# The softplus of a scan step as one ScalarE function on VectorE's copies, in a two-layer state-space and attention block

## The chip, the cores and the metric

The kernel runs on one core of a Trainium2 chip. The metric is the device time of one execution in microseconds (us), the median of several runs. The engines are TensorE (PE in the profile, PEld for its weight loads), VectorE (DVE), ScalarE (ACT), GpSimd (POOL) and SyncE (SP), which only issues DMAs. Each engine works through its own list of instructions in order and waits at an instruction until what it needs is done.

## The reference, cut to what matters

Eight images of 64x64 positions and 96 channels go through two layers. The first is a two-dimensional state-space scan, the second attention without softmax and a feed-forward layer in an emulated 8-bit format. The change lies in the first, in the step sizes of the scan:

```python
xz = x @ in_proj_w.T                               # 192 channels for the scan, 192 for the gate
xc = silu(depthwise 3x3 convolution of the first half)
xs = the image along diagonals and antidiagonals, each also backwards    # 4 directions
dts, Bs, Cs = split(einsum("bkdl,kcd->bkcl", xs, x_proj_weight), [6, 22])
delta = softplus(einsum("bkrl,kdr->bkdl", dts, dt_projs_weight) + dt_projs_bias)
A = -exp(A_logs)                                   # 4 directions x 192 channels x 16 states
def step(h, (u, d, B, C)):
    h = h * exp(d * A) + (d * u) * B               # for each of 16 states
    return h, sum over the states of h * C
y = scans of the four directions, put back into place and added
out = (layernorm(y) * silu(z)) @ out_proj_w.T
```

`delta` is `d`, and `delta * u` is the product that the kernel calls `du`. Softplus is ln(1 + exp(v)). The attention, the feed-forward layer and the norms are computed too, and are not touched.

## The kernel before, in words

**The steps.** A step is one image, one sense (`q`, forwards or backwards) and 512 positions of the scan; both directions of that sense share the 128 partitions, 64 channels each, and three groups (`G = 3`) cover the 192 channels. There are 8 images x 2 senses x 8 chunks = 128 steps. In a step the 16 states are 16 iterations, so the main loop has 2048 iterations; iteration `i` is state `n = i mod 16` of step `m`.

**An iteration.** `decay` makes exp(delta * A) on ScalarE, three activations (L1003), two iterations ahead, into three buffers. The input of the recurrence comes in one of two ways, by the string `FEED = "DADADADADADAAAAA"`. In a D iteration (n = 0, 2, 4, 6, 8, 10) TensorE spreads the row B over the partitions (L1027) and VectorE multiplies it by `du` (three products, L1042). In an A iteration (the other ten) ScalarE multiplies the transposed `du`, called `duT`, by B (eight activations, L1017), and TensorE turns the result (L1025). Both land in the three PSUM banks `feed`. VectorE then runs the recurrence, three scans of 512 positions (L1038). POOL keeps the last column (L1054) and multiplies by C (L1059), and TensorE transposes that product into a PSUM sum (L1073), four iterations after the scan. The `feed` banks are single: a bank is filled for the next iteration after its scan has read it.

**The prologue.** What a step needs beforehand is written by `prologue(m)`: the projections `rows` and `x` (L915 to L928), `delta`, `du` (L966) and `duT` (L971 to L973). It is started at iteration 13 of step m - 2 and runs, spread over the iterations of step m - 1, while that step is scanned. The softplus in it is ln(1 + exp(-|v|)) + max(v, 0): TensorE computes v (L938), ScalarE makes |v|, exp and ln (L940, L942, L945), POOL works out what the sum 1 + e lost by rounding and adds it to the logarithm (four passes, L949, L950, L952, L954), TensorE computes v a second time (L957), and VectorE adds max(v, 0) (L959). `du` has one buffer, so the product waits until iteration 10 of the step before has used its own for the last time.

**The other work.** Beside the scans run, as streams, `front` of the next image (norm, convolution, gate, walk along the diagonals) and `tail` of the last one (join, layer norm, attention, feed-forward). Prologues and streams are Python generators. Before each of their pieces they say which engine it is for and its price in us: `yield act(0.6)`, `dve`, `gp` for POOL, `pe`, and `bank` for TensorE with one of two PSUM banks. The planner `Work` grants each engine a credit an iteration (`PLACES`: ScalarE 2.0, VectorE 1.5, POOL 3.5, TensorE 0.85 three times) and lets a piece in while the credit lasts. A prologue is urgent: it goes in at once and may drive the credit below zero, and the streams then wait. A bank is kept from the streams while a prologue is waiting for one. `LAGS` says how many iterations later a piece may follow one on another engine. All of this is fixed when the program is built; on the chip the order of every engine is a fixed list.

**Tables.** ScalarE has exp and ln in one loaded set of tables. `silu` of the front belongs to another set, so each of its blocks is enclosed by two loads (L566 and, by `k.tables()`, L63).

Of the kernel before, what the change touches and what calls it, by code (L numbers as in the profile page):

```python
# [12 lines left out]
AF = mybir.ActivationFunctionType  # L13
ALU = mybir.AluOpType
# [3 lines left out]
P = 128  # L18
# [6 lines left out]
NR = 6  # L25
# [6 lines left out]
T = 512  # L32
NST = L // T
NSTEP = 2 * NST
TB = T // P
G = 3
# [11 lines left out]
FEED = "DADADADADADAAAAA"  # L48
# [196 lines left out]
def act(us, lag=None):  # L245
    return "A", us, lag, False


def dve(us, lag=None):
    return "V", us, lag, False  # L250


def gp(us, lag=None):
    return "G", us, lag, False


def pe(us, lag=None):
    return "P", us, lag, False


def bank(us, lag=None, long=False):

    return "P", us, lag, "long" if long else "short"
# [130 lines left out]
def view(b, p, *dims):  # L394

    n = int(np.prod(dims))
    v = b[0:p, 0:n]
    if len(dims) == 1:
        return v
    names = "abc"[: len(dims)]  # L400
    return v.rearrange(f"p ({' '.join(names)}) -> p {' '.join(names)}", **dict(zip(names, dims)))
# [458 lines left out]
def run(tc, psum, dram, x, out, w, NB):  # L860
# [9 lines left out]
    nc = tc.nc  # L870
# [24 lines left out]
    made, decays, feeds, hs, carry, sums, other = {}, {}, {}, {}, {}, {}, {}  # L895
    feed = [psum.tile([P, T], F32, tag=f"feed{g}", name=f"feed{g}") for g in range(G)]
    banks = [psum.tile([P, T], F32, tag=f"bank{i}", name=f"bank{i}") for i in range(2)]
    work = Work(banks + feed)

    def prologue(m):  # L900

        b, q, c = steps[m]
        o, u = made[m], made[m].u

        def tile(name, shape, bufs=2):
            return pool.tile(shape, F32, tag=name, name=f"{name}_{m}", bufs=bufs)


        ps = yield bank(1.0, 0)
        v = view(ps, P, TB, NX)  # L910
        for j in range(TB):
            if j == 2:
                yield pe(0.8)
            for g in range(G):
                nc.tensor.matmul(  # L915
                    v[:, j, :], u[:, g, j * P : (j + 1) * P], w.wx[:, q, g, :], start=(g == 0), stop=(g == G - 1)
                )
        yield act(0.45)
        rows = o.rows = tile("rows", [P, TB, NX])
        nc.scalar.copy(rows, v)  # L920
        work.release(ps)
        ps = yield bank(0.45)
        v = view(ps, NX, T)
        for j in range(TB):
            nc.tensor.transpose(v[:, j * P : (j + 1) * P], rows[:, j, :], w.ident)
        yield act(0.6)
        x = o.x = tile("x", [NX, T])
        nc.scalar.activation(x, v, AF.Identity, bias=w.xb)  # L928
        work.release(ps)
        o.crow = dram.tile([2 * NS, T], F32, tag="crow", name=f"crow_{m}", bufs=3)  # L930
        nc.sync.dma_start(out=o.crow, in_=x[XC:NX, :])

        e = tile("e", [P, G, T], 1)
        for g in range(G):
            ps = yield bank(0.85)
            nc.tensor.matmul(ps, w.ws[:, q, g, :], x[0 : 2 * NR + 1, :], start=True, stop=True)  # L938
            yield act(0.6)
            nc.scalar.activation(e[:, g, :], ps, AF.Abs)  # L940
            work.release(ps)
        nc.scalar.activation(e, e, AF.Exp, scale=-1.0)  # L942
        yield act(1.5, 1)
        delta = tile("delta", [P, G, T])
        nc.scalar.activation(delta, e, AF.Ln, bias=w.one)  # L945
        duT = tile("duT", [P, TB * G, P])
        f = duT.rearrange("p (g k) t -> p g (k t)", g=G)
        yield gp(3.0)
        nc.gpsimd.tensor_scalar(f, e, 1.0, 1.0, ALU.mult, ALU.add)  # L949
        nc.gpsimd.tensor_scalar(f, f, -1.0, 1.0, ALU.add, ALU.mult)  # L950
        yield gp(3.4, 1)
        nc.gpsimd.tensor_tensor(e, e, f, ALU.subtract)  # L952
        yield gp(3.4, 1)
        nc.gpsimd.tensor_tensor(delta, delta, e, ALU.add)  # L954
        for g in range(G):
            ps = yield bank(0.85)
            nc.tensor.matmul(ps, w.ws[:, q, g, :], x[0 : 2 * NR + 1, :], start=True, stop=True)  # L957
            yield dve(0.7)
            nc.vector.scalar_tensor_tensor(delta[:, g, :], ps, 0.0, delta[:, g, :], ALU.max, ALU.add)  # L959
            work.release(ps)  # L960
        o.delta = delta
        yield gp(3.4)
        while m and not made[m - 1].multiplied:
            yield "G", 0.0, -1, False
        du = o.du = tile("du", [P, G, T], 1)
        nc.gpsimd.tensor_tensor(du, delta, u, ALU.mult)  # L966
        for j in range(G):
            ps = yield bank(0.45)
            for i in range(4):
                r, g = divmod(4 * j + i, G)  # L970
                nc.tensor.transpose(ps[:, i * P : (i + 1) * P], du[:, g, r * P : (r + 1) * P], w.ident)  # L971
            yield act(0.6)
            nc.scalar.copy(duT[:, 4 * j : 4 * j + 4, :], view(ps, P, 4, P))  # L973
            work.release(ps)
        o.duT = duT

    def bring(m):

        b, q, c = steps[m]
        work.finish(lambda: c in image(b).walked)  # L980
        u = pool.tile([P, G, T], F32, tag="u", name=f"u_{m}", bufs=2)
        made[m] = SimpleNamespace(u=u, c={}, multiplied=False)
        for d in range(2):
            nc.sync.dma_start(
                out=u[d * GC : (d + 1) * GC],
                in_=image(b).seq[d][:, c * T : (c + 1) * T].rearrange("(g i) t -> i g t", i=GC),
            )
# [41 lines left out]
    def recur(i):  # L1029
        m, n = divmod(i, NS)  # L1030
        _, q, _ = steps[m]
        h = hs[i] = pool.tile([P, G, T], F32, tag="h", name=f"h_{i}", bufs=6)
        a = decays.pop(i)
        back = slice(None, None, -1) if q else slice(None)

        def scan(g):
            init = carry[m - 1][:, n, g : g + 1] if m % NST else 0.0
            nc.vector.tensor_tensor_scan(h[:, g, back], a[:, g, back], feed[g][:, back], init, ALU.mult, ALU.add)  # L1038

        if FEED[n] == "D":  # L1040
            for g in (1, 2, 0):
                nc.vector.tensor_tensor(feed[g], feed[0], made[m].du[:, g, :], ALU.mult)  # L1042
        if n == FEED.rindex("D"):
            made[m].multiplied = True
        scan(0)
        scan(1)
        work.at("V")
        scan(2)
# [108 lines left out]
    for m in range(2):  # L1157
        bring(m)
    work.start(prologue(0), urgent=True)
    work.hurry(lambda: not work.urgent)  # L1160

    work.kept = feed
    work.finish(lambda: all(any(f is x for x, _ in work.free) for f in feed))
    work.free = [f for f in work.free if any(f[0] is b for b in banks)]

    work.start(prologue(1), urgent=True)
    for tag, at in (("P", 2), ("A", 0), ("P", 2)):
        work.now += tag == "A"
# [12 lines left out]
    for i in range(total + LAG + 1):  # L1181
        m, n = divmod(i, NS)
# [17 lines left out]
        if i < total:  # L1200
            recur(i)
        else:
            work.at("V")
# [100 lines left out]
```

## Time and profile before

| what | value |
|---|---|
| median of 3 runs | 11828.1 us (11826.46 to 11834.27) |
| profiled execution, its own time | 11827.4 us |
| its span in the trace | 11825.6 us |
| mean granted clock of TensorE | 0.915 |
| first scan starts, last scan ends | 255.5 us, 11567.6 us |
| busy, share of the span: PE, DVE, ACT, POOL | 84%, 82%, 80%, 82% |
| four rounding passes on POOL (L949, L950, L952, L954), busy | 194.0 + 188.8 + 442.0 + 441.1 us |
| VectorE's part of the softplus (L959), busy and idle before it | 259.8 and 257.6 us |
| ScalarE's part (L940, L942, L945), busy | 224.0 + 190.2 + 200.0 us |
| second computation of v (L957), TensorE busy | 440.9 us |

Busy times of an engine are unions, so instructions that overlap count once. The idle time in front of an instruction is put down to what released it. A busy TensorE is not TensorE at its peak, since its matmuls overlap and their ends are modelled.

### The profile page before, as it was taken

The page shows a single profiled execution, that of the slowest core. Times are in us where ns is not written, and L with a number is a line of the kernel's source. Part 1 is how long each engine was busy: PE and PEld are TensorE (multiplying, and loading weights), DVE is VectorE, ACT ScalarE, POOL GpSimd, SP SyncE. Part 2 cuts the span into 40 slices and gives each one's busy share as a digit, 9 for nine tenths or more (in the row PEclk, how much of TensorE's full clock was granted, in tenths as well). Part 3 has the DMA queues.
Part 4 walks back from the last instruction along what each step waited for, and adds up shares of the span by engine and source line. Part 5 has one row for each costly group of instructions (what it writes and reads, how often), then busy time and mean ns, then how long its engine had stood idle before and what let it go on. Part 6 is the DMA issues. An engine that isn't in the chain of part 4 may idle for free.

```text
span 11825.6 us, 186556 instructions
## 1 busy us (share of the span) xinstructions
PE 9882.5 (84%) x62677; PEld 7958.3 (67%) x62677; DVE 9688.2 (82%) x11100; ACT 9489.7 (80%) x19827; POOL 9737.8 (82%) x6927
## 2 busy tenths in 40 slices
PE   6898889888898888888888888988889888888885
PEld 5677677666776667776677666766667666666664
DVE  2988988888888888888888888888888878878993
ACT  3888888878887788887888878887788878878883
POOL 1987988888978898888987889888898878979993
PEclk8999999998998989999898999999999999988996
DMA  3335332533335333353333433344333533332332
GB/s 88 101 93 137 99 93 89 138 107 99 91 93 142 104 95 92 100 136 100 92 96 105 126 101 98 92 118 120 98 92 91 136 104 93 101 92 82 95 96 58
DMA packets 1122756, 1207.21 MB, mean 102 GB/s; under 512 B 452789, under 2 KB 730006, under 8 KB 1121798
## 3 DMA queue, kind: packets, MB, share of 16 engines
q1 hardware_dynamic: 1121798, 1195.28, 36.8%
q8 instruction: 498, 8.16, 0.3%
q14 instruction: 460, 3.77, 0.1%
HBM read 874.83 MB, written 319.98 MB: 101 GB/s over the span
## 4 chain that ended last, share of the span: by engine, by line
PE 33%; DVE 21%; ACT 20%; POOL 11%; issue 8%; DMA 4%; SPq 3%; DVEq 0%; POOLq 0%; ACTq 0%
DVE h L1038 13%; PE y L1073 8%; PE feed L1025 8%; ACT feedT L1017 7%; POOL h L1059 6%; ACT decay L1003 5%; DVE feed L1042 5%; PE bank L550 4%; DMA cc<-crow 2%; PE bank L915 2%; PE bank L957 2%; SPq L595 2%; PE feed L1027 1%; POOL delta L954 1%; PE bank L938 1%
## 5 line engine op out<-in xcount | busy, mean ns | idle before, releaser
L1059 POOL TENSOR_TENSOR h<-h,cc 128x1536 f32<-128x1536 f32 x2048 | 7072.1, 3453 | 364.6 <-DMA cc<-crow 175.3
L1038 DVE TENSOR_TENSOR_SCAN h<-decay,carry,feed 128x512 f32<-128x512 f32 x5376 | 6503.0, 1261 | 634.0 <-PE feed L1025 527.4
L1003 ACT ACTIVATE decay<-delta,a_neg 128x512 f32<-128x512 f32 x6144 | 3977.2, 713 | 1251.7 <-DVE h L1038 1245.6
L1025 PE MATMUL feed<-ident,feedT 128*128 128x128 f32 x15360 | 2744.0, 303 | 1508.2 <-DVE h L1038 1247.0
L1073 PE MATMUL y<-ident,h 128*128 128x128 f32 x24576 | 3805.6, 290 | 69.5 <-ACT ys L1101 37.2
L1017 ACT ACTIVATE feedT<-duT,rows 128x192 f32<-128x192 f32 x10240 | 3671.1, 444 | 2.0 <-PE feed L1025 1.2
L1073 PEld LDWEIGHTS y<-ident,h 128*128 128x128 f32 x24576 | 3153.0, 151 | 528.6 <-issue 477.8
L1025 PEld LDWEIGHTS feed<-ident,feedT 128*128 128x128 f32 x15360 | 1975.1, 155 | 2105.0 <-DVE h L1038 659.3
L1042 DVE TENSOR_TENSOR feed<-feed,du 128x512 f32<-128x512 f32 x2304 | 1442.1, 686 | 215.2 <-PE feed L1027 210.4
L1054 POOL COPY carry<-h 128x3 f32<-128x3 f32 x2048 | 395.6, 193 | 1078.2 <-DVE h L1038 977.3
L1038 DVE TENSOR_TENSOR_SCAN h<-decay,feed 128x512 f32<-128x512 f32 x768 | 883.8, 1202 | 91.9 <-PE feed L1025 75.4
L550 PE MATMUL bank<-wf,xp 97*128 97x192 f32 x4266 | 859.8, 333 | 0.0
L1027 PE MATMUL feed<-x,pick 77*128 77x512 f32 x1536 | 846.2, 633 | 0.6
L550 PEld LDWEIGHTS bank<-wf,xp 97*128 97x128 f32 x4266 | 692.8, 195 | 26.6 <-issue 15.9
L959 DVE SCALAR_TENSOR_TENSOR delta<-bank,delta 128x512 f32<-128x512 f32 x383 | 259.8, 679 | 257.6 <-PE bank L957 136.1
L966 POOL TENSOR_TENSOR du<-delta,u 128x1536 f32<-128x1536 f32 x128 | 449.6, 3513 | 14.1 <-DVE delta L959 14.1
L952 POOL TENSOR_TENSOR e<-e,duT 128x1536 f32<-128x1536 f32 x128 | 442.0, 3453 | 17.5 <-ACT delta L945 17.4
L938 PE MATMUL bank<-x,ws 13*128 13x512 f32 x764 | 438.2, 654 | 15.8 <-ACT x L928 15.8
L954 POOL TENSOR_TENSOR delta<-delta,e 128x1536 f32<-128x1536 f32 x128 | 441.1, 3446 | 0.1
L957 PE MATMUL bank<-x,ws 13*128 13x512 f32 x766 | 440.9, 656 | 0.0
L1027 PEld LDWEIGHTS feed<-x,pick 77*128 77x128 f32 x1536 | 260.9, 201 | 152.0 <-issue 88.7
L949 POOL TENSOR_SCALAR duT<-e 128x1536 f32<-128x1536 f32 x128 | 194.0, 1515 | 202.8 <-ACT e L942 202.8
(287 smaller groups left out, 8921.9 us busy)
## 6 DMA issues: line engine op xcount, KB each, us to landing
cc<-crow SPq DMA_DIRECT2D x4096, 128.0 KB
u<-seq SPq DMA_DIRECT2D x256, 384.0 KB
wide<-ys SPq DMA_DIRECT2D x512, 192.0 KB
ut<-image SPq DMA_DIRECT2D x768, 64.0 KB
seq<-us SPq DMA_DIRECT2D x128, 384.0 KB
part<-ys SPq DMA_DIRECT2D x64, 768.0 KB
y<-part SPq DMA_DIRECT2D x64, 768.0 KB
y<-wide SPq DMA_DIRECT2D x256, 192.0 KB
```

What stands on the lines that cost most here:

```text
L550: nc.tensor.matmul(v[:, j, :], flat[:, o : o + P], k.wf[:, i, :], start=(i == 0), stop=(i == 8), skip_group_check=True)
L938: nc.tensor.matmul(ps, w.ws[:, q, g, :], x[0 : 2 * NR + 1, :], start=True, stop=True)
L954: nc.gpsimd.tensor_tensor(delta, delta, e, ALU.add)
L957: nc.tensor.matmul(ps, w.ws[:, q, g, :], x[0 : 2 * NR + 1, :], start=True, stop=True)
L1003: nc.scalar.activation(decays[i][:, g, :], made[m].delta[:, g, :], AF.Exp, scale=w.a_neg[:, q, g, n : n + 1])
L1017: nc.scalar.activation(f[part], o.duT[part], AF.Copy, scale=scale)
L1025: nc.tensor.transpose(feed[g][:, j * P : (j + 1) * P], feeds[i][:, j * G + g, :], w.ident)
L1027: nc.tensor.matmul(feed[0], w.pick[:, FEED[:n].count("D"), :], made[m].x, start=True, stop=True)
L1038: nc.vector.tensor_tensor_scan(h[:, g, back], a[:, g, back], feed[g][:, back], init, ALU.mult, ALU.add)
L1042: nc.vector.tensor_tensor(feed[g], feed[0], made[m].du[:, g, :], ALU.mult)
L1059: nc.gpsimd.tensor_tensor(hs[i], hs[i], c.unsqueeze(1).to_broadcast([P, G, T]), ALU.mult)
L1073: nc.tensor.matmul(y[:, j, :], hs[i][:, g, r * P : (r + 1) * P], w.ident, is_transpose=True, start=(n == 0 and j % 4 == 0), stop=(n == NS ...
```

## The change

The softplus becomes one activation. VectorE copies v from PSUM to `delta` (three copies), and ScalarE applies its own softplus function to the whole tile in place. That function is in another set of tables, so the compiler puts a load before it, and `w.tables()` loads the old set again after it. The four POOL passes, the second computation of v, |v|, exp, ln and VectorE's max-and-add go. `du` gets two buffers, and the wait for the step before goes with it, along with the flag `multiplied`; `duT` is no longer scratch space. The prices given to the planner change with it.

```diff
-        e = tile("e", [P, G, T], 1)
+        delta = tile("delta", [P, G, T])
         for g in range(G):
             ps = yield bank(0.85)
             nc.tensor.matmul(ps, w.ws[:, q, g, :], x[0 : 2 * NR + 1, :], start=True, stop=True)
-            yield act(0.6)
-            nc.scalar.activation(e[:, g, :], ps, AF.Abs)
+            yield dve(0.6)
+            nc.vector.tensor_copy(delta[:, g, :], ps)
             work.release(ps)
-        nc.scalar.activation(e, e, AF.Exp, scale=-1.0)
-        yield act(1.5, 1)
-        delta = tile("delta", [P, G, T])
-        nc.scalar.activation(delta, e, AF.Ln, bias=w.one)
-        duT = tile("duT", [P, TB * G, P])
-        f = duT.rearrange("p (g k) t -> p g (k t)", g=G)
-        yield gp(3.0)
-        nc.gpsimd.tensor_scalar(f, e, 1.0, 1.0, ALU.mult, ALU.add)
-        nc.gpsimd.tensor_scalar(f, f, -1.0, 1.0, ALU.add, ALU.mult)
-        yield gp(3.4, 1)
-        nc.gpsimd.tensor_tensor(e, e, f, ALU.subtract)
-        yield gp(3.4, 1)
-        nc.gpsimd.tensor_tensor(delta, delta, e, ALU.add)
-        for g in range(G):
-            ps = yield bank(0.85)
-            nc.tensor.matmul(ps, w.ws[:, q, g, :], x[0 : 2 * NR + 1, :], start=True, stop=True)
-            yield dve(0.7)
-            nc.vector.scalar_tensor_tensor(delta[:, g, :], ps, 0.0, delta[:, g, :], ALU.max, ALU.add)
-            work.release(ps)
+        yield act(4.1)
+        nc.scalar.activation(delta, delta, AF.Softplus)
+        w.tables()
         o.delta = delta
         yield gp(3.4)
-        while m and not made[m - 1].multiplied:
-            yield "G", 0.0, -1, False
-        du = o.du = tile("du", [P, G, T], 1)
+        du = o.du = tile("du", [P, G, T])
         nc.gpsimd.tensor_tensor(du, delta, u, ALU.mult)
+        duT = tile("duT", [P, TB * G, P])
...
-        made[m] = SimpleNamespace(u=u, c={}, multiplied=False)
+        made[m] = SimpleNamespace(u=u, c={})
...
-        if n == FEED.rindex("D"):
-            made[m].multiplied = True
```

## The prediction

> **What bounds the kernel now.** I read the page's busy line, then VectorE's waits, then stretches of the scan part, then timelines inside single steps.
>
> ```profile
> PE 9882.5 (84%) x62677; PEld 7958.3 (67%) x62677; DVE 9688.2 (82%) x11100; ACT 9489.7 (80%) x19827; POOL 9737.8 (82%) x6927
> ```
>
> No engine is full. The stretches (span, then busy us and count of PE, PEld, DVE, ACT, POOL) are steps 0 to 7 of image 3, where the next front runs, one late step of the last image with no stream, and the whole scan part:
>
> ```profile
> 4450.20:5132.80 682.60, 596.62 (x3787) 489.07 (x3786) 581.74 (x590) 584.88 (x1187) 572.42 (x303) 0.93 0.40 112
> 11201.30:11276.60 75.30, 65.14 (x407) 50.29 (x406) 69.95 (x69) 66.00 (x141) 70.78 (x38) 0.93 0.35 99
> 255.50:11567.60 11312.10, 9588.58 (x61119) 7725.39 (x61120) 9576.45 (x10744) 9358.49 (x19589) 9636.91 (x6640) 0.92 0.37 103
> ```
>
> The step without streams takes 75.3 us, 69.95 of them on VectorE, whose scans depend on each other through the single `feed` banks. VectorE is the pacemaker; a step lasts VectorE's work plus its idle time. That idle time in the scan part is 11312.1 - 9576.5 = 1736 us, 13.6 us a step. Whatever the change brings must come out of it, out of VectorE's own work, or from ahead of 255.5 us. VectorE's waits over the whole span:
>
> ```profile
> DVE h L1038 <- PE feed L1025: 602.8, 476, 5.7
> DVE feed L1042 <- PE feed L1027: 210.4, 239, 11.3
> DVE st L675 <- ACT y L672: 162.6, 75, 5.0
> DVE delta L959 <- POOL delta L954: 151.0, 23, 35.4
> DVE delta L959 <- PE bank L957: 136.1, 133, 2.5
> ```
>
> The fourth line is the rounding: 35.4 us of it is the start, 115.6 falls in the scans. Most of that is one place per image, step 6, iteration 7; here for image 3, POOL and then VectorE:
>
> ```profile
> 4990.06 3.44 POOL L1059 TENSOR_TENSOR h<-h,cc 128x1536 f32<-128x1536 f32 x1 [14.92 <-DMA cc<-crow]
> 4993.48 1.47 POOL L949 TENSOR_SCALAR duT<-e 128x1536 f32<-128x1536 f32 x1
> ...
> 5007.13 3.42 POOL L954 TENSOR_TENSOR delta<-delta,e 128x1536 f32<-128x1536 f32 x1
> ...
> 5010.57 0.69 DVE L959 SCALAR_TENSOR_TENSOR delta<-bank,delta 128x512 f32<-128x512 f32 x1 [13.52 <-POOL delta L954]
> ```
>
> POOL got C late, its passes slid back, and VectorE stood at L959 with all scans behind it. The first line of the list, TensorE late with `feed`, sits largely at the end of the A run, n = 14 and 15. In the step without streams, ScalarE is busy without a gap from 11253.4 to 11272.7 (4.8 us an A iteration, decay 1.94 plus feedT 2.87, against 3.6 of scans), and VectorE loses 2.13 + 0.59 + 0.70 = 3.4 us:
>
> ```profile
> 11264.94 0.57 ACT L973 COPY duT<-bank 128x512 f32<-128x512 f32 x1
> ...
> 11267.20 2.45 DVE L1038 TENSOR_TENSOR_SCAN h<-decay,carry,feed 128x512 f32<-128x512 f32 x2 [2.13 <-PE feed L1025]
> ```
>
> **What the Trainium skill says.** "ScalarE: Activation LUTs", section "What ACT_TABLE_LOAD costs", prices a switch at about 1283 ns for the load plus about 1380 ns of drain. The trace agrees with the first and not the second:
>
> ```profile
> 3140.26 1.28 ACT L566 ACT_TABLE_LOAD   x1
> 3141.56 0.84 ACT L566 ACTIVATE pre<-pre 128x768 f32<-128x768 f32 x1
> 3142.31 1.04 ACT L567 ACTIVATE z<-z 96x1024 f32<-96x1024 f32 x1
> 3143.37 1.28 ACT L63 ACT_TABLE_LOAD   x1
> 3144.66 1.49 ACT L1017 ACTIVATE feedT<-duT,rows 128x192 f32<-128x192 f32 x4
> ```
>
> Work follows 0.02 us after each load, so I use 1.283. The page's section "Step-by-step: what each stage is for" says throughput doesn't depend on the function; here exp takes 1486 ns and ln with a pointer bias 1562 on 128x1536. Softplus is not in the trace; I take 1.49, the row of exp (below by nothing, above 2 x 1.49 if it needed two passes). "VectorE: DVE Perf Modes", section "Why PSUM operands drop a tier", says an fp32 operand in PSUM holds VectorE to one element a cycle. So a copy gains nothing over the max-and-add: L959 takes 679 ns, the PSUM copies of L536 also 679 on 96x512.
>
> **The change part by part.** The built order of instructions gives places. In most steps |v| stood in iterations 0 to 2, exp in 2, ln in 3, the POOL passes in 3 to 5, L957 and L959 in 6 to 9, `du` in 10, the `duT` copies in 12 to 14. Now the VectorE copies stand in 0 to 2, the softplus with both loads in 3, `du` in 3, the `duT` copies in 5 to 7. Loads go from 129 to 385, two per step.
>
> Busy sums a step. POOL: 1265.9 / 128 = 9.9 us less. TensorE: 440.9 / 128 = 3.4 us less as modelled. ScalarE: 614.2 / 128 = 4.80 out, 2 x 1.283 + 1.49 = 4.06 in, 0.74 less. VectorE: equal. SP issues the same DMAs. None of that is time yet; on the pacemaker:
>
> 1. *Start.* The first prologue is serial: the third v is ready at 228.05, `du` begins at 242.40. New: copy 0.7, softplus 1.5 (its load waits for nothing and runs before), hops 0.1, so `du` at 230.4. **-12 us**.
> 2. *VectorE's wait for the rounding*, 115.6 us. What is late next in step 6 is POOL's product for TensorE's sums; with 9.9 us of passes gone the products follow every 3.7 us, and TensorE waited 0.4 us for the first of them. **-100** (bounds -85, -116).
> 3. *VectorE's wait for L957*, 136.1, mostly 0.86 us in iteration 7, where TensorE does L957 after the skip matmuls (L1080) of iterations 5 to 7 in backward steps. The remaining v matmuls stand at the ends of iterations 15, 0 and 1, clear of these. **-90** (0 to -130).
> 4. *End of the A run.* `duT`'s three copies (0.47 us each after overlap, 1.4) leave ScalarE, and twelve transposes (L971, 1.3 us) leave TensorE. Both chains are gapless there. 1.3 x 128 = **-166** (-60 to -250; more than the 3.4 us a step isn't there).
> 5. *The lump in iteration 3.* decay 1.94, loads and softplus 4.06, feedT 2.87: 8.9 us after scan(2), while TensorE can first fill `feed` for iteration 5 at 3.5 + 2.1 + 1.2 = 6.8 us and VectorE needs it at 9.1. Filling adds 0.5, so 0.3 to 0.4 us is lost: **+50** (0 to +150 where ScalarE comes in late). The softplus waits for the third copy, made in iteration 2, but decay(5) ahead of it waits for that iteration's scans anyway. POOL's `du` waits about 1 us for the softplus, with only its own product behind it; three iterations pass before TensorE needs that: 0. If that cover were gone it would be 1 us a step.
> 6. *The other side of 5.* In steps 1 to 5 of an image VectorE now loses some 2 us in iteration 5 because |v|, exp and ln sit there beside the silu blocks. About 1 us in 40 steps: **-40** (0 to -80).
> 7. *TensorE in those steps*, 597 of 683 us busy: 3.4 us less work each, of which I count 1 us in 40 steps: **-40** (0 to -100).
>
> Second buffer of `du`, freed scratch: nothing alone; they permit 4. Freed credits let streams run about half a step earlier; their work is the same, so 0 (-80 to +80). Sum: -12 - 100 - 90 - 166 + 50 - 40 - 40 = -398. From the profiled execution's 11827.4, near the median 11828.1, about **11430 us**. This case's own range is 11270 to 11600.
>
> **The rivals.**
> *POOL counts more.* The chain of waits gives POOL 11%, and in the tail's steps 13 to 15 of image 3 it is busy 248 of 270 us. If those 24 steps lose 6 us more each, and waits for VectorE statistics behind POOL's norms shrink alike in steps 8 to 11 (32 x 4), that is 144 + 128 = 270 more: 11160. Against it: the whole list of VectorE's waits names POOL at L959 and hardly elsewhere.
> *Little reaches the pacemaker.* Only 1 and 2 hold; 4 is eaten by stream pieces that the planner puts where `duT` was, and 3 reappears at the copies. -112 + 50: about 11765. No change within 0.2% would need step 2 to be replaced by another stall at step 6.
> *Slower: the lump.* If softplus and two switches hold ScalarE longer, iteration 5 waits every step. With the skill's drains, 2 x 1.38 more, the loss in 5 grows from 0.4 to 3.1 us; step by step it decides from 0.4 + 398 / 128 = 3.5 us, that is 3.1 us of lateness. A two-pass softplus on top (1.5) would give 128 x 4.2 = 540 more: 11970. Against it: the 0.02 us after the loads seen above, and ScalarE's idle time of 4.2 us in iteration 8 of the late step.
> That the loads are merged or the passes stay is excluded by the built order.
>
> **How the numbers follow.** Changes within 0.2% (24 us) can't be told from none. Main case 0.66, POOL rival 0.14, little 0.13 (0.03 of it within 0.2%), lump 0.07. So faster 0.90, same 0.03, slower 0.07. The range leaves out the lump, the end of the little case and the far end of the POOL case: 11220 to 11720.
>
> **What would show it.** L959's successor should have no wait for POOL; iteration 7 of step 6 (first scan to next first scan, 4994.6 to 5014.3 in image 3) should fall from 19.7 us to under 8; VectorE's busy time should stay near 9690 and its idle time in the scans fall to about 1350; the late step should take some 73.5 us; the first scan should start near 243.5. ScalarE should follow each load within 0.1 us, and softplus take 1.5 us. I am wrong if VectorE waits at iteration 5 for feedT by more than 1 us in most steps, or if softplus is dearer than exp.

## The result and the profile after

| | before | after |
|---|---|---|
| median | 11828.9 us (4 runs, 11826.46 to 11834.27) | 11735.0 us (4 runs, 11719.27 to 11742.83) |
| ratio, 95% interval | | 0.9918 (0.9901 to 0.9935) |
| span of the profiled execution | 11825.6 us | 11741.0 us |
| first scan starts, last scan ends | 255.5, 11567.6 us | 243.7, 11478.8 us |
| scan part, VectorE idle in it | 11312.1, 1736 us | 11235.1, 1655 us |

The change makes the kernel 94 us faster, 0.8%. I had forecast 398 us, so the sign is right and three quarters of the gain is missing; the time is 15 us above the upper end of my range. The two profiled executions, 85 us apart, say where it came: 11.8 us at the start, 77 in the scans, and 4 lost behind them.

The page's busy line of the kernel after:

```profile
PE 9593.9 (82%) x61909; PEld 7953.8 (68%) x61909; DVE 9692.3 (83%) x11100; ACT 9433.7 (80%) x19571; POOL 8495.7 (72%) x6415
```

POOL lost 1242 us of work, TensorE 289, ScalarE 56, and VectorE has what it had. For POOL and VectorE that is as worked out; TensorE was to lose 441, ScalarE 95. VectorE's work being equal, the time must be looked for in VectorE's idle time. The stretches of after (span, then busy us and count of PE, PEld, DVE, ACT, POOL) are the whole scan part, steps 0 to 7 of image 3, and the late step of the last image without a stream:

```profile
243.70:11478.80 11235.10, 9301.12 (x60356) 7719.44 (x60357) 9580.34 (x10744) 9302.99 (x19335) 8404.59 (x6132) 0.91 0.38 104
4430.10:5133.90 703.80, 596.81 (x3784) 504.62 (x3784) 585.80 (x605) 587.37 (x1182) 498.43 (x283) 0.91 0.39 108
11180.90:11258.80 77.90, 63.83 (x401) 51.44 (x400) 70.27 (x70) 65.86 (x139) 61.30 (x34) 0.89 0.34 96
```

Two of them got longer: the late step takes 77.9 us (its neighbours 76.4 to 77.7) instead of 75.3, where I had expected 73.5, and the first half of image 3 takes 703.8 instead of 682.6. The gain lies in the second halves. For the mean of images 1 to 6, steps 0 to 7 go from 683.5 to 703.0 and steps 8 to 15 from 759.4 to 726.2. VectorE's waits in after:

```profile
DVE h L1020 <- PE feed L1007: 812.3, 601, 11.0
...
DVE st L675 <- ACT y L672: 56.3, 55, 5.2
DVE delta L939 <- PE bank L937: 54.1, 43, 19.6
```

The wait for POOL at the softplus, 151.0 us before, is gone, and the wait for the second v, 136.1, has become 54.1 at the copies, of which 19.6 is the start. The third line fell too, from 162.6, which I had not forecast; it is a statistic of the tail, and with the softplus one iteration later (below) it is back at 119.6, so it seems to go with the places of the streams. The first line is the loser: scans that wait for `feed` went from 602.8 to 812.3 us. To see where, I summed from both traces the idle time before VectorE's instructions by the iteration in which it falls, from the first scan to the last, us per step, all 128 steps:

| iteration n | 1 | 3 | 5 | 7 | 9 | 13 | 14 | 15 | all 16 |
|---|---|---|---|---|---|---|---|---|---|
| before | 0.97 | 0.70 | 1.64 | 1.75 | 0.48 | 0.88 | 1.12 | 3.11 | 13.56 |
| after | 0.32 | 0.26 | **3.16** | 0.82 | 0.20 | 0.30 | **3.20** | 1.72 | 12.93 |

Iterations 1, 3, 7, 9 and 13 gained 2.9 us a step together, more than the removed waits for POOL and the second v alone. Iteration 5 lost 1.5 us a step. Iteration 14 lost 2.1 and iteration 15 gained 1.4, so the end of the A run got longer in sum, not shorter. Iteration 5 in the late step, ScalarE first:

```profile
11196.41 1.95 ACT L985 ACTIVATE decay<-delta,a_neg 128x512 f32<-128x512 f32 x3 [4.13 <-DVE h L1020]
11198.38 1.28 ACT L942 ACT_TABLE_LOAD   x1
11199.67 1.49 ACT L942 ACTIVATE delta<-delta 128x1536 f32<-128x1536 f32 x1
11201.17 1.28 ACT L63 ACT_TABLE_LOAD   x1
11202.47 2.87 ACT L999 ACTIVATE feedT<-duT,rows 128x192 f32<-128x192 f32 x8
11205.25 1.47 ACT L1086 COPY ys<-y 128x768 f32<-128x768 f32 x2
```

The loads and the softplus have exactly the prices I used: 4.09 us, nothing between them. The last line copies the sums `y` of the step before out of PSUM; it belongs to iteration 3 and stands behind feedT. Then VectorE, the three scans and the products after them:

```profile
11205.98 1.28 DVE L1020 TENSOR_TENSOR_SCAN h<-decay,carry,feed 128x512 f32<-128x512 f32 x1 [0.55 <-PE feed L1007]
11208.86 1.28 DVE L1020 TENSOR_TENSOR_SCAN h<-decay,carry,feed 128x512 f32<-128x512 f32 x1 [1.61 <-PE feed L1007]
11210.57 1.28 DVE L1020 TENSOR_TENSOR_SCAN h<-decay,carry,feed 128x512 f32<-128x512 f32 x1 [0.43 <-PE feed L1007]
11212.61 1.90 DVE L1024 TENSOR_TENSOR feed<-feed,du 128x512 f32<-128x512 f32 x3 [0.75 <-PE feed L1009]
```

The first scan is late by 0.55 us, near the 0.3 to 0.4 that I had worked out. But three more waits follow, and the four make 3.3 us (2.3 to 4.1 in the neighbouring steps). What TensorE did at that time, and six microseconds later:

```profile
11203.32 0.33 PE L1007 MATMUL feed<-ident,feedT 128*128 128x128 f32 x1 [3.09 <-ACT feedT L999]
...
11206.82 1.09 PE L1053 MATMUL y<-ident,h 128*128 128x128 f32 x4 [0.95 <-issue]
11207.70 1.06 PE L1007 MATMUL feed<-ident,feedT 128*128 128x128 f32 x4
11208.55 1.06 PE L1053 MATMUL y<-ident,h 128*128 128x128 f32 x4
11209.40 1.06 PE L1007 MATMUL feed<-ident,feedT 128*128 128x128 f32 x4
...
11216.52 0.60 PE L1053 MATMUL y<-ident,h 128*128 128x128 f32 x4
11217.14 0.66 PE L1007 MATMUL feed<-ident,feedT 128*128 128x128 f32 x4
11217.63 0.60 PE L1053 MATMUL y<-ident,h 128*128 128x128 f32 x4
```

TensorE had stood idle for 3.09 us. Most of that it waited for the bank, which the first scan of iteration 4 (11201.81 to about 11203.1) still read, and only the last 0.2 us for feedT. From there on two things delay it.

The first is the line with 0.95. The view names no releaser, but in TensorE's queue the instruction ahead of it is released at 11206.73 by the copy L1086 on ScalarE, which ended at 11206.72: the sums of the new step go into the PSUM tile that is being copied. They stand ahead of the second `feed` bank. Over all steps TensorE waits 126 us at this place, against 66 in before; the page of after books 65.3 of the 126 under the same copy in forward steps, L1081.

The second is the pace. Four transposes take 1.06 us, starting 0.85 apart; later four take 0.60 to 0.66, and the starts shown are 0.49 and 0.62 apart. A bank of `feed` needs four, and four of the sums stand between, so the second and third bank came 1.7 us apart while a scan takes 1.2. I had reckoned with one filling at full pace, and with no wait for the copies.

One place does show the change at its best. In step 6 of image 3, iteration 7 was 19.7 us long before; in after the scans of iterations 6 and 7 run through, and iteration 7 takes 5.5 us, under the 8 that I had named (VectorE):

```profile
4997.49 1.90 DVE L1024 TENSOR_TENSOR feed<-feed,du 128x512 f32<-128x512 f32 x3 [1.08 <-PE feed L1009]
4999.51 7.13 DVE L1020 TENSOR_TENSOR_SCAN h<-decay,carry,feed 128x512 f32<-128x512 f32 x6
5006.56 1.87 DVE L1024 TENSOR_TENSOR feed<-feed,du 128x512 f32<-128x512 f32 x3
```

One step earlier there is something new, though. TensorE in step 5 of image 3:

```profile
4937.76 1.09 PE L602 MATMUL bank<-ident,ut 128*128 128x128 f32 x4 [7.27 <-DMA ut<-image]
...
4953.34 5.37 PE L915 MATMUL bank<-wx,u 128*128 128x77 f32 x24 [5.61 <-DMA u<-seq]
```

The streams moved earlier, and the end of the front now stands in iterations 12 and 14 with all matmuls for `feed` queued behind two DMAs; VectorE loses 7.45 and 10.09 us there. Step 5 of images 1 to 6 went from 91.1 to 95.5 us in the mean, step 6 from 89.7 to 78.8: a part of what the rounding gave at step 6 was lost again at step 5.

The same images lose 9.9 us in iteration 14 of step 2 and again of step 3, where before loses 0.6 and nothing. Step 2 of image 3, TensorE and then VectorE:

```profile
4672.69 5.24 PE L915 MATMUL bank<-wx,u 128*128 128x77 f32 x24
```

```profile
4672.15 1.28 DVE L1020 TENSOR_TENSOR_SCAN h<-decay,carry,feed 128x512 f32<-128x512 f32 x1 [4.04 <-PE feed L1007]
4678.90 1.28 DVE L1020 TENSOR_TENSOR_SCAN h<-decay,carry,feed 128x512 f32<-128x512 f32 x1 [5.46 <-PE feed L1007]
```

A silu block of the front with its two loads (4.4 us of ScalarE, from 4664.24) now stands ahead of the feedT of iteration 14, a second lump; TensorE, after several waits for parts of feedT, then takes 5.24 us between two `feed` banks for the 24 projection matmuls of the next prologue, which take 2.80 at best (shown below). These two places cost 113 us more than before over the run.

### The profile page after: what moved, and what is told of

Same layout as the page of the kernel before. It is cut to its first block, busy times and chain, and to the rows that moved or that the text cites. A ratio compares the mean times of both kernels' runs of the same rounds, so it can differ in the third digit from the quotient of the medians.

```text
span 11741.0 us, 184544 instructions
## 1 busy us (share of the span) xinstructions
PE 9593.9 (82%) x61909; PEld 7953.8 (68%) x61909; DVE 9692.3 (83%) x11100; ACT 9433.7 (80%) x19571; POOL 8495.7 (72%) x6415
## 4 chain that ended last, share of the span: by engine, by line
ACT 32%; PE 28%; DVE 27%; issue 5%; SPq 3%; DMA 3%; POOL 2%; DVEq 0%; ACTq 0%; POOLq 0%
DVE h L1020 17%; ACT feedT L999 13%; ACT decay L985 9%; PE y L1053 7%; PE feed L1007 7%; DVE feed L1024 6%; PE bank L915 3%; PE bank L550 3%; ACT L63 2%; SPq L595 2%; ACT delta L942 1%; POOL h L1039 1%; PE feed L1009 1%; ACT L942 1%; DVE delta L939 1%
## 5 line engine op out<-in xcount | busy, mean ns | idle before, releaser
L1007 PE MATMUL feed<-ident,feedT 128*128 128x128 f32 x15360 | 2872.9, 308 | 1710.5 <-DVE h L1020 1178.4
L1053 PE MATMUL y<-ident,h 128*128 128x128 f32 x24576 | 3840.7, 291 | 126.3 <-ACT ys L1081 65.3
L1007 PEld LDWEIGHTS feed<-ident,feedT 128*128 128x128 f32 x15360 | 2018.9, 157 | 2399.0 <-ACT feedT L999 827.0
L947 POOL TENSOR_TENSOR du<-delta,u 128x1536 f32<-128x1536 f32 x128 | 440.9, 3445 | 317.9 <-ACT delta L942 317.9
L915 PE MATMUL bank<-wx,u 128*128 128x77 f32 x3048 | 423.0, 304 | 38.1 <-DMA u<-seq 38.1
L915 PEld LDWEIGHTS bank<-wx,u 128*128 128x128 f32 x3048 | 418.9, 222 | 46.1 <-issue 45.6
L937 PE MATMUL bank<-x,ws 13*128 13x512 f32 x764 | 435.0, 649 | 1.0 <-ACT x L928 1.0
L955 ACT COPY duT<-bank 128x512 f32<-128x512 f32 x383 | 220.1, 575 | 195.9 <-PE bank L953 195.7
L939 DVE COPY delta<-bank 128x512 f32<-128x512 f32 x382 | 256.0, 670 | 54.7 <-PE bank L937 54.1
L953 PE MATMUL bank<-ident,du 128*128 128x128 f32 x1532 | 253.0, 292 | 0.0
```

What stands on the lines that cost most here:

```text
L915: nc.tensor.matmul(v[:, j, :], u[:, g, j * P : (j + 1) * P], w.wx[:, q, g, :], start=(g == 0), stop=(g == G - 1))
L1007: nc.tensor.transpose(feed[g][:, j * P : (j + 1) * P], feeds[i][:, j * G + g, :], w.ident)
L1053: nc.tensor.matmul(y[:, j, :], hs[i][:, g, r * P : (r + 1) * P], w.ident, is_transpose=True, start=(n == 0 and j % 4 == 0), stop=(n == NS ...
```

## The experiments

The theory from these profiles: the lump of 4.06 us, standing between decay and feedT, costs some 3 us in iteration 5 and hides what the early `duT` gives. The rivals: the gain was never there (the softplus could stand anywhere); or the time is lost to streams that the planner put elsewhere.

**The softplus one iteration later.** One number in the planner's table of prices and lags puts it behind the three decays of an iteration whose input is a D product, so no feedT stands behind it.

```diff
-        yield act(4.1)
+        yield act(4.1, 2)
```

> The changed kernel with the softplus and its two loads one iteration later, in iteration 4, a D iteration with no feedT of its own behind it. Theory A (the lump of 4.06 us on ScalarE stands in iteration 3 just ahead of the feedT that iteration 5 needs): VectorE's idle time in iteration 5 falls from 3.2 us a step to under 1, a step without streams from 78 to about 75 us, the kernel from 11735 to 11350 to 11500 us. Theory B (the gain went to the streams, which moved and stall at other places): iteration 5 changes little and the time stays within 60 us of 11735.

Measured: 11330.4 us (11316.21 to 11342.35), ratio to before 0.9577 (0.9562 to 0.9591). That is 405 us less than after and 500 less than before, a little below the range expected. ScalarE in a late step:

```profile
10728.13 1.95 ACT L985 ACTIVATE decay<-delta,a_neg 128x512 f32<-128x512 f32 x3
10730.09 1.28 ACT L942 ACT_TABLE_LOAD   x1
10731.39 1.48 ACT L942 ACTIVATE delta<-delta 128x1536 f32<-128x1536 f32 x1
10732.89 1.28 ACT L63 ACT_TABLE_LOAD   x1
10734.18 1.95 ACT L985 ACTIVATE decay<-delta,a_neg 128x512 f32<-128x512 f32 x3
```

The same four instructions at the same prices, now ahead of a decay that has two iterations to spare. VectorE's idle time in iteration 5 falls from 3.16 to 0.71 us a step, in this late step to nothing. TensorE and then VectorE, for iteration 5 of the same step:

```profile
10728.96 1.09 PE L1007 MATMUL feed<-ident,feedT 128*128 128x128 f32 x4 [3.19 <-ACT decay L985]
10729.84 1.06 PE L1053 MATMUL y<-ident,h 128*128 128x128 f32 x4
```

```profile
10727.53 7.14 DVE L1020 TENSOR_TENSOR_SCAN h<-decay,carry,feed 128x512 f32<-128x512 f32 x6
```

TensorE stands idle as long as in after, 3.19 us, and comes out of it at the same half pace, but the scans of iterations 4 and 5 run without a gap: the first bank is full at 10730.05, a microsecond before its scan, and the sums wait for no copy. So the idle stretch and the pace alone don't make the loss. Over all steps the wait at the first sums is 8 us here, against 126 in after.

The kernel's busy line and its largest wait:

```profile
PE 9388.5 (83%) x61909; PEld 7812.8 (69%) x61909; DVE 9681.7 (85%) x11100; ACT 9413.7 (83%) x19571; POOL 8498.6 (75%) x6415
```

```profile
DVE h L1020 <- PE feed L1007: 461.1, 402, 5.5
```

The same count of instructions on every engine, and 351 us less waiting for `feed`. TensorE's busy time falls by 205 us with the same matmuls: of its transposes for `feed` and `y`, 5357 were 0.15 to 0.3 us ahead of the next of their kind in after, and 4730 are here, the rest mostly 0.11. The stall in step 5 (82.7 us in the mean of images 1 to 6) and the 9.9 us in step 3 are gone here as well, since the planner's order shifted, so the 405 us are not the lump alone; iteration 5 makes 314 of them.

**No loads at all.** This leaves the softplus out: |v| in its place, from the set that is loaded, and no second load. The order of the remaining instructions is that of after.

```diff
-        nc.scalar.activation(delta, delta, AF.Softplus)
-        w.tables()
+        nc.scalar.activation(delta, delta, AF.Abs)
```

> The changed kernel with the absolute value, which needs no other tables, in the place of the softplus, and without the load behind it; it leaves the softplus out, and the order of all other instructions is that of the changed kernel. Theory A: the lump shrinks from 4.06 to 1.49 us, VectorE's idle time in iteration 5 falls from 3.2 to under 0.7 us a step, 2.5 to 3.3 us a step in all, so 11310 to 11420 us. Theory B: the loads are hidden, 11680 to 11735 us.

Measured: 11380.0 us, ratio 0.962 (0.9606 to 0.9634), 355 us less than after. Idle in iteration 5: 0.67. With the order kept, 2.8 us a step less of ScalarE's work (9080.1 us busy against 9433.7) are worth 2.8 us. This is the cleanest measure of what the two loads cost. Against before it is 450 us less.

**Two loads in the kernel before.** The other direction: the lump without the rest of the change.

```diff
+        w.tables()
         nc.scalar.activation(delta, e, AF.Ln, bias=w.one)
+        w.tables()
```

> The kernel before with two loads of the tables it already has, one before and one after the ln of iteration 3; nothing else. ScalarE is held 2.57 us longer there, 1.283 + 1.56 + 1.283 = 4.1 us in one piece, as long as the softplus with its loads. Theory A: VectorE loses 2.5 to 3.3 us a step in iteration 5, the kernel goes from 11828 to 12100 to 12250 us. If ScalarE's idle time in iterations 7 and 8 absorbs it, as I predicted: under 11900 us.

Measured: 12037.1 us against 11836.7 for before, ratio 1.0171 (1.0156 to 1.0186), 200 us more. That is less than the 272 to 422 expected, because iteration 5 of before lost 1.64 us already. VectorE in a late step, iteration 5:

```profile
11422.16 1.28 DVE L1040 TENSOR_TENSOR_SCAN h<-decay,carry,feed 128x512 f32<-128x512 f32 x1 [0.87 <-PE feed L1027]
11425.06 1.28 DVE L1040 TENSOR_TENSOR_SCAN h<-decay,carry,feed 128x512 f32<-128x512 f32 x1 [1.61 <-PE feed L1027]
11426.76 1.28 DVE L1040 TENSOR_TENSOR_SCAN h<-decay,carry,feed 128x512 f32<-128x512 f32 x1 [0.43 <-PE feed L1027]
11428.30 1.90 DVE L1044 TENSOR_TENSOR feed<-feed,du 128x512 f32<-128x512 f32 x3 [0.26 <-PE feed L1029]
```

The same waits one after the other, two of them equal to those of after, and 3.16 us in iteration 5 over all steps, as in after. So two loads around a function of 1.5 us, ln as well as softplus, make the stall when they stand between decay and feedT.

**The kernel before without the rounding.** The four POOL passes and their scratch are left out, so that the part of the logarithm that 1 + e loses is not put back; the order is that of before.

```diff
-        nc.gpsimd.tensor_scalar(f, e, 1.0, 1.0, ALU.mult, ALU.add)
-        nc.gpsimd.tensor_scalar(f, f, -1.0, 1.0, ALU.add, ALU.mult)
...
-        nc.gpsimd.tensor_tensor(e, e, f, ALU.subtract)
...
-        nc.gpsimd.tensor_tensor(delta, delta, e, ALU.add)
```

> The kernel before without its four rounding passes on POOL, everything else in the same order and at the same prices; it leaves out the correction for rounding. My sum put the wait for them at 100 us: 11828 to about 11716 with the 12 us of the start, between 11690 and 11745. If POOL counts more than VectorE's list of waits says: under 11650. If another wait takes its place in step 6: over 11780.

Measured: 11724.6 us, ratio 0.9914 (0.9897 to 0.993), 105 us less, the start included (first scan at 245.9). Steps 1 and 2 of my sum said 112. So 1236 us less work on POOL are worth about its two waits; no sign of a bound by POOL elsewhere.

**The early `duT` taken back.** `du` with one buffer and the old wait for the step before, with the softplus where after has it, and with the softplus one iteration later.

```diff
-        du = o.du = tile("du", [P, G, T])
+        while m and not made[m - 1].multiplied:
+            yield "G", 0.0, -1, False
+        du = o.du = tile("du", [P, G, T], 1)
...
```

> The changed kernel with one buffer for du and the wait for the step before, so that du and duT stand in iterations 10 and 12 to 14 again. My sum put the gain of their earlier place at 166 us (60 to 250): then this takes 11800 to 11985 us. If the end of the A run is bound by ScalarE's decay and feedT alone, and the early copies only move the load to where the lump already is: 11680 to 11760 us.

> The changed kernel with the softplus in iteration 4 (as in the run with 11330 us) and du with one buffer and the wait, so that du and duT stand in iterations 10 and 12 to 14. With the lump out of the way this measures what their earlier place gives. If my 1.3 us a step at the end of the A run is right and only the lump covered it: 11450 to 11580 us. If that end is set by the 24 matmuls of L915 between two fillings of feed, and not by the copies: 11330 to 11400 us.

| median, us | `duT` late | `duT` early | early is worth |
|---|---|---|---|
| softplus in iteration 3 | 11759.4 | 11735.0 (after) | 24 |
| softplus one later | 11525.1 | 11330.4 | 195 |

The first fell where I had expected it if the early copies only move load to the place of the lump, the second in the range of my 166 us. Neither of the two is a clean removal: with the wait back, the planner lets the softplus slip in 30 of some 127 steps of the first and in 37 of the second, and iteration 5 idles 2.20 and 1.38 us a step where its neighbour on the right has 3.16 and 0.71. Taking that difference out (0.96 x 128 = 123 one way, 0.67 x 128 = 86 the other) leaves 147 and 109 us. These are estimates, since other pieces moved too. They bracket no more than the size: my 166 for step 4 is somewhat too high and of the right order, but not where I had put it.

In the late step, iterations 14 and 15 lose 2.60 us in after and with the softplus one later, against 3.42 before. What fills the rest is seen in the variant with the later softplus, first on TensorE and then on VectorE:

```profile
10768.12 0.60 PE L1053 MATMUL y<-ident,h 128*128 128x128 f32 x4
10768.56 2.80 PE L915 MATMUL bank<-wx,u 128*128 128x77 f32 x24
10771.20 0.60 PE L1007 MATMUL feed<-ident,feedT 128*128 128x128 f32 x4
```

```profile
10759.48 10.63 DVE L1020 TENSOR_TENSOR_SCAN h<-decay,carry,feed 128x512 f32<-128x512 f32 x9
10771.91 2.45 DVE L1020 TENSOR_TENSOR_SCAN h<-decay,carry,feed 128x512 f32<-128x512 f32 x2 [1.79 <-ACT feedT L999]
```

The 24 projection matmuls of the next prologue stand in one block between the first and the second `feed` bank of iteration 14. VectorE's wait is put down to ScalarE's feedT, but feedT was ready: TensorE was in that block.

**The prologue started in iteration 15.** The later softplus, and the block moved out of the A run.

```diff
-            if n == NS - 3 and m + 2 < len(steps):
+            if n == NS - 1 and m + 2 < len(steps):
                 work.start(prologue(m + 2), urgent=True)
```

> The changed kernel with the softplus lagging two iterations and the prologue started in iteration 15 and not 13, so that L915 leaves the A run for iterations 15 and 0, and the softplus stands in iteration 6, again a D iteration. If L915 sets the end of the A run, VectorE's idle time in iteration 14 falls from 2.4 to under 1 us a step in the mean and the kernel from 11330 to 11100 to 11230 us. If ScalarE's decay and feedT set it, 11300 to 11360 us.

Measured: **11228.8 us** (11206.4 to 11234.32), ratio 0.9483 (0.9469 to 0.9498), the fastest of all: 506 us less than after. Idle in iteration 14 falls from 2.41 to 1.53 us a step, where I had expected under 1, and in the late step from 1.80 to 0.42.

**The walk's lag doubled.** For the stall in step 5 of after: the piece that needs the DMA of `ut` is let in eight iterations after its issue instead of four.

```diff
-                ps = yield bank(0.45, 4 if g == 0 else 0)
+                ps = yield bank(0.45, 8 if g == 0 else 0)
```

> The changed kernel with TensorE asking for the walk's data eight iterations after the DMA's issue and not four. In the changed kernel TensorE stood 7 us at L602 for ut in iteration 12 of step 5 of six images, and 5.6 us for u two iterations later. If these two are what took the place of the removed wait in step 6, the first goes: 40 to 60 us, 11675 to 11700 us. If the streams only move and stall elsewhere: within 25 us of 11735.

Measured: 11748.9 us, ratio 0.9926 (0.9911 to 0.9941), 14 us more than after: no gain, as expected if the streams only stall elsewhere. TensorE's waits for DMAs in this kernel:

```profile
PE bank L915 <- DMA u<-seq: 89.4, 6, 15.5
...
PE bank L602 <- DMA ut<-image: 27.4, 2, 20.7
```

In after the first of them is 38.1 and the second 80.7 us. The stall moved from one DMA to the next, and VectorE's idle time from iteration 12 (0.80 to 0.47 us a step) to 14 (3.20 to 3.99).

**The second v put back.** Three more matmuls and bank claims at the end of each prologue, their result unused, on the later softplus; it tests step 7, what the lighter TensorE is worth.

```diff
         o.duT = duT
+        for g in range(G):
+            ps = yield bank(0.85)
+            nc.tensor.matmul(ps, w.ws[:, q, g, :], x[0 : 2 * NR + 1, :], start=True, stop=True)
+            yield dve(0.0)
+            work.release(ps)
```

> The changed kernel with the softplus lagging two iterations (11330 us) and the second computation of v put back on TensorE, at the end of the prologue, where nobody reads it: three matmuls a step, their banks and their price to the planner. It measures what their absence gives without VectorE's wait for them. My sum counted 40 us for TensorE's lighter work: 11370 us, up to 11430. If TensorE's load doesn't reach VectorE's pace: 11320 to 11345 us.

Measured: 11765.9 us, ratio 0.9937 (0.9921 to 0.9954), 436 us more than without. My 40 is far off, but this is not the matmuls' own time. VectorE's waits of this kernel have a line that after has at 24.3 us:

```profile
DVE hq L840 <- ACT h L837: 112.6, 29, 20.8
```

The three pieces take credits and banks from the streams, and the tail isn't done when the image ends; the loop then finishes it at once with the scans standing (47.1 us in one iteration of image 3). Step 0 takes some 117 us against 72 in images 2 to 6 and 104 against 79 in image 7, together 252 of the 436. What TensorE's work alone costs stays open.

**silu away from the A run.** The starting prologue of the fastest variant, and silu blocks let in only in iterations 0, 1, 2, 7, 8 and 9.

```diff
+            while not work.alone and work.n not in (0, 1, 2, 7, 8, 9):
+                yield SPIN
```

> The kernel with the prologue started in iteration 15 (11229 us), in which the silu blocks of the front, 4.4 us of ScalarE with two loads each, may be placed only in iterations 0 to 2 and 7 to 9, where D and A iterations alternate. If a ScalarE block of that length costs some 3 us wherever a feedT is due behind it, and less in the alternating part than in the A run: 64 blocks, of which about half stood in iterations 12 to 14, give 50 to 120 us, 11110 to 11180 us. If the place doesn't matter: 11210 to 11240 us; if the front is held up by the gate: over 11240 us.

Measured: 11277.0 us, ratio 0.9524 (0.9508 to 0.954), 48 us more than the variant that it changes: a miss. Iteration 3, to which no silu block may go, idles 1.14 us instead of 0.48; the cause stays open.

**TensorE kept busy ahead of iteration 5.** 24 transposes without use in front of the `feed` of iteration 5, whenever a bank is free when the program is built.

```diff
+        if n == 5 and g == 0 and work.free:
+            for _ in range(24):
+                nc.tensor.transpose(work.free[0][0][:, 0:P], w.ident, w.ident)
```

> The changed kernel (11735 us) with 24 transposes of the identity into an idle PSUM bank, which nobody reads, put in TensorE's list just ahead of the filling of feed for iteration 5, where it otherwise stands idle for some 3 us behind the lump. If most of the lump's price is that TensorE comes out of that idle time at half its pace and then fills three banks at 1.7 us apart and not 0.9: VectorE's idle time in iteration 5 of a step without streams falls from 3.3 to about 1 us, and the kernel to 11550 to 11660 us, in spite of 2.6 us more work on TensorE a step. If only feedT's lateness counts: 11720 to 11850 us.

Measured: 11900.6 us, ratio 1.0058 (1.0041 to 1.0075), 166 us slower than after and beyond both ranges expected. TensorE in a late step:

```profile
11290.74 2.78 PE L1007 MATMUL bank<-ident 128*128 128x128 f32 x24
11294.20 0.33 PE L1010 MATMUL feed<-ident,feedT 128*128 128x128 f32 x1 [0.68 <-ACT feedT L999]
...
11297.69 1.09 PE L1056 MATMUL y<-ident,h 128*128 128x128 f32 x4 [1.09 <-issue]
11298.57 1.06 PE L1010 MATMUL feed<-ident,feedT 128*128 128x128 f32 x4
```

The idle stretch of 3.09 us became one of 0.68, but waits for parts of feedT and 1.09 us for the copy L1089 (the copy of the sums in this kernel) follow it, and the transposes were slow all the same; iteration 5 of this late step idled 2.78 us. In steps with streams the useless transposes waited for banks, in order, with `feed` behind them, and over all steps iteration 5 rose to 4.55 us.

The traces still divide the loss in part. In some steps of this run the first bank is filled piece by piece as feedT comes and the sums wait for the copy, as in after, but the second and third bank are filled at full pace. The same step of different images can then be compared: in step 15, iteration 5 loses 1.08 us with both at full pace (images 1 to 5) and 2.94 and 2.99 with one at half pace (images 0 and 6); in step 6 it is 1.8 (images 2 to 4) and 3.36 (images 1, 5 and 6). With the softplus one iteration later, 33 steps have both banks at half pace but neither delay, and lose 0.42 in the mean. So ScalarE's lateness alone costs 1 to 2 us, half pace adds 1.6 to 1.9 to it, and costs little where ScalarE is in time. These are steps compared, not a removal.

## Why the prediction was right and wrong, step by step

**The failed step is 5, the lump in iteration 3.** I said +50 us, and up to +150 where ScalarE comes in late. Its lateness at the first scan was right (0.55 us measured, 0.3 to 0.4 worked out), and so were the prices: 1.28 us for each load, 0.02 between a load and the function after it, 1.485 for the softplus. What I left out is what follows the first scan. I added one filling at full pace, 0.5 us, and put the second and third at nothing. But the lump also holds up ScalarE's copies of the last step's sums, for which TensorE waits ahead of the second bank (0.95 us in the late step, 126 us over the run), and TensorE works at half pace after its idle time, which it had slack for only while ScalarE was in time. The loss is 3.3 us in the late step and 3.16 over all steps, where before has 1.64. That is +195 us by iteration 5's idle time, +200 by adding two loads to the kernel before, and 355 us by taking the loads from after. The last is larger because it takes away more than the difference to before: |v|, exp and ln had a cost there too.

This one term, 355 us where I had 50, is as large as the whole miss: without the loads the changed kernel is 450 us below before, and my sum without step 5 was 448. That the other terms met so well in sum is luck, as the list shows.

**The rest of the sum.**
1. *Start*: -12 said, -11.8 measured. Right.
2. *Rounding*: right. Steps 1 and 2 together were -112, the run without the passes gave -105; the 317.9 us that POOL's `du` now waits for the softplus cost nothing that I can find, since POOL idles for VectorE's scans by the thousand.
3. *The wait for the second v*: 136.1 us became 34.5 in the scans, -102 for a forecast of -90. This is read from the waits alone; no run takes it by itself, and with the softplus one iteration later the copies wait 113.4 us again.
4. *End of the A run*: -166 said; an estimate of -110 to -150 by the two runs without it, and not at the A run's end, where the late step gained 0.8 us of the 1.3 and iterations 12 to 15 gained 9 us over the run. I took both chains there as gapless and did not look at what else stood in TensorE's: the block of 24 projection matmuls, 2.8 us, which became the next limit.
5. See above.
6. *The other side of 5*, -40: hidden in after, where iteration 5 rose. Without the loads iteration 5 idles 0.67 us against 1.64 before, 125 us over the run and 79 in the 40 steps that I meant, so the place was right and the gain larger than I had said.
7. *TensorE in the front's steps*, -40: not seen. Those steps got longer, from 683.5 to 703.0 us, by the lump and the new stalls in an image's steps 2, 3 and 5. How much the lighter TensorE gives is open.

I had put moved streams at 0 (-80 to +80). The new stall in an image's step 5 takes 17.5 us in image 3, though the step as a whole lost only 4.4 against before, and iteration 14 of steps 2 and 3 takes 113 us more over the run; what the moved streams cost on balance I could not separate. The planner's reaction to small edits (48 us by gating silu, 252 of the 436 us by three bank claims) shows that this term deserved more width.

**The rivals.** "Little reaches the pacemaker" has the nearest time, 11765, and mostly the wrong reason. Its steps 1 and 2 hold, but so does 3, which it gave up, and the early `duT` was not simply eaten; a larger lump ate the sum. Stream pieces did move into iteration 14. "Slower: the lump" named the right place and loss (3.1 us a step with its drains, 3.16 measured), yet by drains and a two-pass softplus, neither of which the trace shows; and it would have turned the sign only from 3.5 us of added loss, by the sum above. I listed "VectorE waits at iteration 5 for feedT by more than 1 us in most steps" as what would prove me wrong. It did, although the trace books most of it under `feed`. "POOL counts more" falls with the run without the rounding.

## What to carry to other kernels

When a block is put on an engine ahead of work that feeds the pacemaker, count not only how late the first piece comes. Count what else stands behind the block on its own engine, here the copies of the sums, and what the engine in between must still deliver, at the pace it has after standing idle, before it has caught up. Look for the place where the block has slack before giving up on it: one number in the planner was worth four times the whole change (405 us against 94). And when a chain is called gapless, list everything in it; after the named parts left, the next block in the list was the limit, and starting the prologue two iterations later gave another 102 us.

## What the runs showed of the hardware

Softplus took 1485 ns on 128x1536 (1482 to 1493 in 128 instances), the same as exp (1486), so no second pass. Work follows 0.02 us after a load of tables, in this place too.

TensorE's pace goes with its recent idleness. In the trace of before, I counted the 128x128 transposes that start 1 to 2 us after an idle stretch of TensorE, with no other idle stretch above 0.1 us between: 18% were slow (over 150 ns to the next start) after idle stretches of 0.3 to 0.7 us, 85% after 2.6 to 3.2 us, 99% after 3.2 to 4.5 us. Of those that start 5 to 6 us after such a stretch, 0 to 4% were. The Trainium skill, "TensorE: Matmul & The Clock Gate", section "What's actually happening", gives half the clock after an idle window of about 3.4 us and full clock after about as long a busy one. The traces agree in kind, with half the pace often reached after less (3.09 us in the late step). What this pace costs depends on the slack: nothing in the late step with the softplus one iteration later, 1.6 to 1.9 us a step by the comparison above where ScalarE is late too.
